# Gate of a quantised feed forward by tanh, one chunk pair at a time, and its weights rounded in pieces

## The chip, the cores and the metric

The kernel runs on one core of one Trainium2 chip. The metric is the device time of one execution in microseconds (us), lower is better. Each version is run several times and the median counts. The engines are TensorE (PE in the profile, with its weight loads as PEld), VectorE (DVE), ScalarE (ACT), GpSimd (POOL) and SyncE (SP), which here only issues transfers. Every engine works through its own instructions strictly in order and waits for others by semaphores.

## The reference, cut to what matters

Six blocks transform `x` of shape (4, 1024, 256), each followed by a residual add and a layer norm: self attention, cross attention and a feed forward in layer 0, then the same three kinds in layer 1. The change touches the feed forward of layer 0 alone:

```python
def act_quant(x):
    scale = 127.0 / jnp.clip(jnp.max(jnp.abs(x), axis=-1, keepdims=True), 1e-05)
    return jnp.clip(jnp.round(x * scale), -128, 127) / scale

def weight_quant(w):
    scale = 1.0 / jnp.clip(jnp.mean(jnp.abs(w)), 1e-05)
    return jnp.clip(jnp.round(w * scale), -1, 1) / scale
...
h = bit_linear(x, w1)                       # 256 -> 1024, both sides rounded
h = depthwise_conv1d(h.transpose(0, 2, 1), conv_w, conv_b)   # 3 taps along the sequence
h = h.transpose(0, 2, 1)
h = jax.nn.silu(h)
return bit_linear(h, w2)                    # 1024 -> 256, both sides rounded
```

So for each batch element `b`: the 1024 tokens are rounded with one scale per token, multiplied by a ternary weight, convolved along the sequence for each of the 1024 hidden channels, gated by silu, rounded again with one scale per token (the largest absolute value over the 1024 channels) and multiplied by a second ternary weight. silu(h) = h * sigmoid(h) = (h/2) * (1 + tanh(h/2)).

## The kernel before, in words

**Stages.** From 0 to about 780 us runs the self attention of layer 0, from there to about 1480 us its cross attention, to about 1890 us the self attention of layer 1, and then layer 1's cross attention and feed forward. The feed forward of layer 0 has no stage of its own. It is laid between the work of two others: batch elements 0 and 1 inside the cross attention (`wide_cross_attention`), 2 and 3 mostly inside the self attention of layer 1 (`wide_self_attention`).

**Order of the work.** Each stage collects events, `at(when, function, ...)`, sorts them by `when` and calls them. In the cross attention one unit of `when` is one call of `scores` (L706, L710 and L714: the maximum, four exponentials, the reciprocal; then the normalising on POOL, L718 and L721). Everything that goes to TensorE is pinned to this order (`pe`, `mm`); so are transfers that go through `pe`. Other instructions are placed by a planner: it issues what it expects to be ready, in its own estimate of time, and may move an early-ready instruction ahead of others on its engine. Once placed, the order on each engine is fixed.

**Weights.** `weight_quant` loads a weight as 128 x 2048 float32 (L616, into the slot `gt`, of which there is one), sums absolute values (L618, DVE), adds over the partitions with a matmul (L620, PE), takes the scale (L622, L624) and rounds to -1, 0 or 1 in three steps: L625 and L626 on DVE, L627 on POOL. It runs as one event at 20.5 for the first weight and at 36.5 for the second. The second load needs the slot that the first rounding leaves.

**Feed forward.** `schedule` spreads a batch element over a length of 38 to 40 units in four quarters `r` of 256 tokens. In `hidden(r, m)`, `m` from 0 to 3, TensorE makes two chunks of 128 channels; DVE takes them out of PSUM with the token scales (`ht`, L882, two buffers); for each chunk ACT does the middle tap with bias (L889) and DVE the two outer taps on 255 columns (L892, L895). `gated(r)` does the whole quarter at once: it adds the neighbours' taps at the two edges (L903, L905, from `ed` made in `edge_tokens`), takes silu of 128 x 2048 (L906, ACT) and the largest absolute value over the eight chunks (L908, DVE). `hidden_scales` turns these maxima (L915, PE) and makes scales (L917, L802 to L807); `quantised_hidden` multiplies and rounds (L923, L927, L930); `fed_forward` multiplies by the second weight. The quarter lies in the one slot `gt`, from `hidden` to L930.

In the stretches that the feed forward lies in, other ACT work is mostly exponentials: L710 in cross attention and L1036 in self attention. DVE's other work there is chiefly the maxima L706 and L1034 and the copies out of PSUM, L736, L1048.

Of the kernel before, what the change touches and what calls it, by code (L numbers as in the profile page):

```python
# [8 lines left out]
F32 = mybir.dt.float32  # L9
# [20 lines left out]
def decoder_kernel(ctx: ExitStack, tc: tile.TileContext, a: dict, out: bass.AP):  # L30
# [558 lines left out]
    def wide_cross_attention(wk, wf, slot, bank):  # L589
# [21 lines left out]
        def weight_quant(name):  # L611


            w = wf.tile([P, 8, E], F32, tag="gt", name="wf", bufs=1).rearrange("p c n -> p (c n)")
            src = a[name].rearrange("(c p) n -> p c n", p=P)
            nc.sync.dma_start(out=w.rearrange("p (c n) -> p c n", c=src.shape[1]), in_=src)  # L616
            asum = small.tile([P, 1], F32, tag="asum", name="asum")
            nc.vector.tensor_reduce(asum, w, AX.X, ALU.add, apply_absolute_value=True)  # L618
# [4 lines left out]
            sc = small.tile([P, 1], F32, tag="wsc", name="wsc")  # L623
# [3 lines left out]
            nc.gpsimd.tensor_scalar(wq.rearrange("p c n -> p (c n)"), w, -1.0, 0.0, ALU.max, ALU.add)  # L627
# [136 lines left out]
        at(20.5, weight_quant, "L0_ffn_w1")  # L764
        at(36.5, weight_quant, "L0_ffn_w2")
# [23 lines left out]
    def feed_forward(wf, bank):  # L789
# [4 lines left out]
        scs, dqs, xqTs, rows, edges, gts, ams, sc2s, dq2s, gqs, sts = ({} for _ in range(11))  # L794
# [52 lines left out]
        def edge_tokens(b):  # L847
# [3 lines left out]
            for hc in range(8):  # L851
# [3 lines left out]
            ed = edges[b] = wf.tile([P, 8, 3, 2], F32, tag="ed", name="ed", bufs=1)  # L855
# [3 lines left out]
                ed.rearrange("p c q n -> p c (q n)"),  # L859
# [3 lines left out]
            for n in range(2):  # L863
                nc.vector.tensor_tensor(
                    ed[:, :, :, n], ed[:, :, :, n],
                    cw[:, :, 2 * n : 2 * n + 1].to_broadcast([P, 8, 3]), ALU.mult,
                )

        def hidden(b, r, m):
            if m == 0:  # L870
                gts[b, r] = wf.tile([P, 8, N], F32, tag="gt", name="gt", bufs=1)
            g2 = gts[b, r]
            t = bank()
            for i in range(2):
# [709 lines left out]
```

## Time and profile before

| what | value |
|---|---|
| median of 3 runs | 2347.14 us (2345.06 to 2352.85) |
| the profiled execution | 2353.62 us, of which the profile's span is 2351.9 us |
| PE busy | 2202.1 us, 94% of the span |
| DVE busy | 1471.0 us, 63% |
| ACT busy | 1110.5 us, 47% |
| POOL busy | 504.6 us, 21% |
| mean granted TensorE clock | 0.957 of full speed |

The page's second part cuts the span into 40 slices and gives each engine's busy share in tenths; `PEclk` is the clock that was granted to TensorE. The table by stretches gives, for each stretch, its length, then busy us and the number of instructions for PE, PEld, DVE, ACT and POOL, then the granted clock, the share of the DMA engines and GB/s. A row of instruction groups reads: line, engine, operation, output<-input by the program's names, shapes, count | busy us in total, mean ns of one | idle time of the engine just before them and what ended it. In the time line, a row is start, duration, engine, line, operation, names, shapes, count, and in brackets the idle time before it. Matmul ends are modelled, so a busy PE can still be a PE that runs below its peak.

### The profile page before, as it was taken

How to read it: one execution, taken by the hardware profiler on the slowest of the kernel's cores; microseconds unless marked ns; L12 is line 12 of the kernel's file. 1: busy time of each engine (PE TensorE's matmuls, PEld its weight loads, DVE VectorE, ACT ScalarE, POOL GpSimd, SP SyncE). 2: the span in 40 equal slices, each digit the busy share in tenths (PEclk: the TensorE clock that was granted, in tenths of full speed). 3: DMA queues.
4: the chain of work that ended last, by engine and by line, in shares of the span. 5: the costliest groups of instructions: out<-in, count | busy, mean ns of one | idle time of the engine just before them, and what ended most of it. 6: DMA issues, size and time to landing. Idle time of an engine off the chain costs nothing.

```text
span 2351.9 us, 37670 instructions
## 1 busy us (share of the span) xinstructions
PE 2202.1 (94%) x14228; PEld 1288.3 (55%) x14228; DVE 1471.0 (63%) x3113; ACT 1110.5 (47%) x2699; POOL 504.6 (21%) x1111
## 2 busy tenths in 40 slices
PE   7999999999999999999889988889899999999996
PEld 4444544454444556556556555656666655555645
DVE  5666666666665654557787787775874365645544
ACT  1455554554555464445655654334543334444444
POOL 1111111111111464544334333000000021111102
PEclk9999999999999999999989988999999999999998
DMA  3201200000000100000000000000000010010101
GB/s 91 51 6 33 55 5 15 10 15 15 9 12 1 37 19 1 1 1 1 1 1 1 32 1 21 1 1 1 1 0 1 1 20 12 12 28 12 30 1 36
DMA packets 24437, 34.76 MB, mean 15 GB/s; under 512 B 5952, under 2 KB 19648, under 8 KB 24256
## 3 DMA queue, kind: packets, MB, share of 16 engines
q1 hardware_dynamic: 22640, 31.20, 5.8%
q8 instruction: 113, 1.85, 0.3%
q10 hardware_dynamic: 1616, 1.16, 0.2%
q14 instruction: 68, 0.56, 0.1%
HBM read 15.56 MB, written 4.19 MB: 8 GB/s over the span
## 4 chain that ended last, share of the span: by engine, by line
PE 74%; DVE 16%; ACT 7%; issue 1%; DMA 1%; POOL 1%; SPq 0%; ACTq 0%; DVEq 0%; POOLq 0%
PE s L178 22%; PE t L568 16%; PE s L1138 10%; PE s L568 9%; PE acc L178 6%; PE acc L1138 3%; PE t L735 2%; ACT u L710 2%; DVE gt L892 2%; DVE gt L895 2%; DVE x L156 1%; DVE bnst L136 1%; DVE am L908 1%; DVE nmp L319 1%; ACT gt L906 1%
## 5 line engine op out<-in xcount | busy, mean ns | idle before, releaser
L385 ACT ACTIVATE p<-s 128x512 f32<-128x512 f32 (+1 forms) x640 | 319.4, 554 | 297.4 <-PE s L178 294.7
L319 DVE TENSOR_REDUCE nmp<-s 128x1 f32<-128x512 f32 (+3 forms) x640 | 298.9, 524 | 155.7 <-PE s L178 155.7
L178 PE MATMUL s<-qs,kp 32*128 32x512 f32 (+3 forms) x1536 | 370.5, 532 | 2.7 <-DVE nmp L319 2.7
L178 PE MATMUL s<-kp,qp 32*128 32x128 f32 (+3 forms) x2304 | 329.5, 408 | 5.6 <-DVE nmp L319 3.5
L718 POOL TENSOR_SCALAR p<-u,rs 128x128 f32<-128x128 f32 x512 | 201.3, 411 | 339.1 <-DVE rs L714 242.9
L178 PEld LDWEIGHTS s<-kp,qp 32*128 32x128 f32 x2304 | 167.7, 188 | 142.9 <-issue 43.5
L388 POOL TENSOR_SCALAR_AFFINE_SELECT p<-p 128x256 f32<-128x256 f32 x256 | 100.6, 408 | 650.8 <-ACT p L385 650.8
L710 ACT ACTIVATE u<-s,nmx 128x154 f32<-128x154 f32 x512 | 192.1, 389 | 62.0 <-DVE nmx L706 50.5
L178 PEld LDWEIGHTS s<-qs,kp 32*128 32x128 f32 x1536 | 143.8, 187 | 65.4 <-DVE nmp L319 28.0
L141 POOL TENSOR_TENSOR rstd<-ve,neghalf 128x4 f32<-128x4 f32 (+1 forms) x56 | 54.7, 977 | 549.7 <-DVE ve L139 514.4
L178 PE MATMUL acc<-p,v 128*32 128x512 f32 (+3 forms) x1536 | 165.4, 511 | 1.1 <-ACT ot L427 0.8
L568 PEld LDWEIGHTS s<-kt,qt 64*128 64x128 f32 x1024 | 106.9, 194 | 77.7 <-issue 58.4
L568 PE MATMUL s<-kt,qt 64*128 64x154 f32 x1024 | 141.5, 325 | 2.1 <-ACT u L710 1.8
L706 DVE TENSOR_REDUCE nmx<-s 128x4 f32<-128x616 f32 x128 | 101.5, 793 | 62.5 <-PE s L568 62.0
L568 PE MATMUL t<-xT,xw 128*128 128x512 f32 x256 | 128.9, 628 | 4.0 <-DVE xT L638 3.7
L1295 DVE TENSOR_REDUCE nmt<-s 128x3 f32<-128x462 f32 (+1 forms) x192 | 99.0, 579 | 46.5 <-PE s L1138 46.5
L568 PE MATMUL t<-xw,ot 128*128 128x256 f32 x512 | 119.2, 387 | 4.3 <-DVE pt L736 3.8
L568 PE MATMUL t<-v,pt 128*128 128x256 f32 x512 | 117.9, 383 | 5.2 <-DVE pt L1048 3.8
L568 PE MATMUL s<-qt,xT 128*128 128x512 f32 x256 | 117.7, 603 | 0.0
L335 DVE TENSOR_REDUCE nmp<-s 128x4 f32<-128x512 f32 x128 | 82.6, 688 | 49.6 <-PE s L178 49.6
L568 PEld LDWEIGHTS t<-v,pt 128*128 128x128 f32 x512 | 96.8, 192 | 26.9 <-issue 5.7
L568 PEld LDWEIGHTS t<-xw,ot 128*128 128x128 f32 x512 | 96.8, 194 | 18.1 <-DVE pt L736 4.3
(255 smaller groups left out, 3898.6 us busy)
## 6 DMA issues: line engine op xcount, KB each, us to landing
qp<-sq SPq DMA_DIRECT2D x128, 64.0 KB, 2.3
kp<-sk SPq DMA_DIRECT2D x64, 64.0 KB, 2.3
out_dram<-x SPq DMA_DIRECT2D x8, 512.0 KB, 2.9
x<-in_x_dram SPq DMA_DIRECT2D x3, 1024.0 KB, 5.4
wf<-in_L_ffn_w_dram SPq DMA_DIRECT2D x2, 1024.0 KB, 5.2
xw<-in_L_xattn_wk_dram SPq DMA_DIRECT2D x1, 1024.0 KB, 5.3
xw<-in_L_xattn_wq_dram SPq DMA_DIRECT2D x1, 1024.0 KB, 5.8
xw<-in_L_xattn_wv_dram SPq DMA_DIRECT2D x1, 1024.0 KB, 5.1
```

Of the source, the lines that this page charges most:

```text
L141: nc.gpsimd.tensor_tensor(rstd[:, :n], ve[:, :n], neghalf[:, :n], ALU.pow)
L178: pe(nc.tensor.matmul(o, l, r, start=start, stop=stop))
L319: nc.vector.tensor_reduce(nmp[:, 2 * pair + g, qc, i : i + 1], t[g][:, c0 : c0 + n], AX.X, ALU.max)
L335: nc.vector.tensor_reduce(nmp[:, 2 * pair + g, q0 : q0 + 4, 0], t[g].rearrange("p (j n) -> p j n", j=4), AX.X, ALU.max,)
L385: nc.scalar.activation(p[:, g, :total], t[g][:, :total], AF.Exp)
L388: nc.gpsimd.affine_select(out=v, in_=v, compare_op=ALU.is_ge, fill=0.0, base=0, pattern=[[0, 2], [1, P]], channel_multiplier=-1,)
L568: pe(nc.tensor.matmul(o, l, r, start=start, stop=stop))
L706: nc.vector.tensor_reduce(nmx.rearrange("p i g -> p g i"), t, AX.X, ALU.max, negate=True)
L710: nc.scalar.activation(u[:, 2 * i + g, :], t[:, g, i, :], AF.Exp, bias=nmx[:, i, g : g + 1], accum_out=ssum[:, i, g : g + 1],)
L718: nc.gpsimd.tensor_scalar(p[:, h * P : (h + 1) * P], u[:, h, :P], rs[:, h : h + 1], 1.0, ALU.mult, ALU.mult)
L1138: pe(nc.tensor.matmul(o, l, r, start=start, stop=stop))
L1295: nc.vector.tensor_reduce(nmts[s % 2][:, 3 * u : 3 * u + n, g, 17], ts[g][:, : n * LK].rearrange("p (c k) -> p c k", k=LK), AX.X, ALU.max, ...
```

## The change

Four things change, all in the feed forward of layer 0.

1. **Weights.** `weight_quant` becomes four functions. The load is pinned in order on SP (events 12.6 and 28.6 instead of 20.5 and 36.5). The sum is four pieces of 512 columns, the mean adds four columns of PSUM, and the rounding is four pieces of three instructions, all on DVE; POOL has no part in it. Sums, mean and pieces have events of their own, one unit apart.
2. **Edges.** `ed` becomes ten columns per chunk (the neighbours of each quarter's two edges, with zeros at the ends of the sequence), cleared by POOL once per batch element. ACT copies two of them to the sides of each `ht`, which grows by two columns, so the convolution's outer taps run over all 256 columns and the edge additions (L903, L905) and the products L864 go.
3. **Gate.** The taps and bias are halved once. ACT takes tanh of each chunk pair at the end of `hidden`; `gated(r, m)`, one and a half steps later, does (tanh + 1) * g on DVE, an absolute value on ACT and a running maximum on DVE, with one more maximum of the two halves after the last pair. `ht` is kept as the place for tanh and the absolute value, so it is held until that pair's maximum. The maxima move from the slot `am` into the slot `xq`.
4. **Times.** For batch elements 2 and 3 the four `hidden` calls are 2.0 instead of 1.6 hundredths of the length apart.

```diff
-        def weight_quant(name):
...
-            nc.sync.dma_start(out=w.rearrange("p (c n) -> p c n", c=src.shape[1]), in_=src)
-            asum = small.tile([P, 1], F32, tag="asum", name="asum")
-            nc.vector.tensor_reduce(asum, w, AX.X, ALU.add, apply_absolute_value=True)
-            t = bank()
-            pe(nc.tensor.matmul(t[:, 0:1], ones, asum, start=True, stop=True))
-            wq, mean = quantised[name]
-            nc.vector.tensor_scalar(mean, t[:, 0:1], 1.0 / (P * 2048), 1e-5, ALU.mult, ALU.max)
+        floats = {}
+        def weight_loaded(name):
             w = wf.tile([P, 8, E], F32, tag="gt", name="wf", bufs=1).rearrange("p c n -> p (c n)")
...
+            pe(nc.sync.dma_start(out=w.rearrange("p (c n) -> p c n", c=src.shape[1]), in_=src))
+            asum = small.tile([P, 4], F32, tag="asum", name="asum")
             sc = small.tile([P, 1], F32, tag="wsc", name="wsc")
+            floats[name] = w, asum, sc
+        def weight_sum(name, i):
+            w, asum, _ = floats[name]
+            nc.vector.tensor_reduce(
+                asum[:, i : i + 1], w[:, i * 512 : (i + 1) * 512], AX.X, ALU.add, apply_absolute_value=True
+            )
+        def weight_mean(name):
+            _, asum, sc = floats[name]
+            t = bank()
+            pe(nc.tensor.matmul(t[:, 0:4], ones, asum, start=True, stop=True))
+            _, mean = quantised[name]
+            nc.vector.tensor_reduce(mean, t[:, 0:4], AX.X, ALU.add)
+            nc.vector.tensor_scalar(mean, mean, 1.0 / (P * 2048), 1e-5, ALU.mult, ALU.max)
             nc.vector.reciprocal(sc, mean)
+        def weight_quant(name, i):
+            w, _, sc = floats[name]
+            w = w[:, i * 512 : (i + 1) * 512]
+            wq = quantised[name][0].rearrange("p c n -> p (c n)")[:, i * 512 : (i + 1) * 512]
             nc.vector.tensor_scalar(w, w, sc, RND, ALU.mult, ALU.add)
             nc.vector.tensor_scalar(w, w, RND, 1.0, ALU.subtract, ALU.min)
-            nc.gpsimd.tensor_scalar(wq.rearrange("p c n -> p (c n)"), w, -1.0, 0.0, ALU.max, ALU.add)
+            nc.vector.tensor_scalar(wq, w, -1.0, 0.0, ALU.max, ALU.add)
...
-        at(20.5, weight_quant, "L0_ffn_w1")
-        at(36.5, weight_quant, "L0_ffn_w2")
+        for t0, name in ((12, "L0_ffn_w1"), (28, "L0_ffn_w2")):
+            at(t0 + 0.6, weight_loaded, name)
+            at(t0 + 9.6, weight_mean, name)
+            for i in range(4):
+                at(t0 + 5.6 + i, weight_sum, name, i)
+                at(t0 + 10.6 + i, weight_quant, name, i)
...
+        nc.vector.tensor_scalar(cw, cw, 0.5, None, ALU.mult)
+        nc.vector.tensor_scalar(cb, cb, 0.5, None, ALU.mult)
...
-            ed = edges[b] = wf.tile([P, 8, 3, 2], F32, tag="ed", name="ed", bufs=1)
+            ed = edges[b] = wf.tile([P, 8, 2 * Q + 2], F32, tag="ed", name="ed", bufs=1)
+            nc.gpsimd.memset(ed, 0.0)
...
-            for n in range(2):
-                nc.vector.tensor_tensor(
-                    ed[:, :, :, n], ed[:, :, :, n],
-                    cw[:, :, 2 * n : 2 * n + 1].to_broadcast([P, 8, 3]), ALU.mult,
-                )
...
-            ht = wf.tile([P, 2, N], F32, tag="ht", name="ht", bufs=2)
+            ht = wf.tile([P, 2, N + 2], F32, tag="ht", name="ht", bufs=2)
             nc.vector.tensor_tensor(
-                ht, t.rearrange("p (i n) -> p i n", i=2),
+                ht[:, :, 1 : N + 1], t.rearrange("p (i n) -> p i n", i=2),
...
+            for c, k in ((0, 2 * r), (N + 1, 2 * r + 3)):
+                nc.scalar.copy(ht[:, :, c : c + 1], edges[b][:, 2 * m : 2 * m + 2, k : k + 1])
+            g2 = gts[b, r][:, 2 * m : 2 * m + 2, :]
             for i in range(2):
                 hc = 2 * m + i
-                g = g2[:, hc, :]
+                g = g2[:, i, :]
                 nc.scalar.activation(
-                    g, ht[:, i, :], AF.Identity, bias=cb[:, hc : hc + 1], scale=cw[:, hc, 1:2]
+                    g, ht[:, i, 1 : N + 1], AF.Identity, bias=cb[:, hc : hc + 1], scale=cw[:, hc, 1:2]
                 )
-                nc.vector.scalar_tensor_tensor(
-                    g[:, 1:], ht[:, i, : N - 1], cw[:, hc, 0:1], g[:, 1:], ALU.mult, ALU.add
-                )
-                nc.vector.scalar_tensor_tensor(
-                    g[:, : N - 1], ht[:, i, 1:], cw[:, hc, 2:3], g[:, : N - 1], ALU.mult, ALU.add
-                )
-        def gated(b, r):
-            g = gts[b, r]
-            if r > 0:
-                nc.vector.tensor_tensor(g[:, :, 0], g[:, :, 0], edges[b][:, :, r - 1, 0], ALU.add)
-            if r < Q - 1:
-                nc.vector.tensor_tensor(g[:, :, N - 1], g[:, :, N - 1], edges[b][:, :, r, 1], ALU.add)
-            nc.scalar.activation(g, g, AF.Silu)
-            am = ams[b, r] = wf.tile([P, N], F32, tag="am", name="am", bufs=1)
-            nc.vector.tensor_reduce(
-                am, g.rearrange("p c n -> p n c"), AX.X, ALU.max, apply_absolute_value=True
-            )
+                for k in (0, 2):
+                    nc.vector.scalar_tensor_tensor(
+                        g, ht[:, i, k : k + N], cw[:, hc, k : k + 1], g, ALU.mult, ALU.add
+                    )
+            nc.scalar.activation(ht[:, :, :N], g2, AF.Tanh)
+            ths[b, r, m] = ht
+        def gated(b, r, m):
+            g2 = gts[b, r][:, 2 * m : 2 * m + 2, :]
+            th = ths.pop((b, r, m))
+            nc.vector.scalar_tensor_tensor(g2, th[:, :, :N], 1.0, g2, ALU.add, ALU.mult)
+            if m == 0:
+                ams[b, r] = wf.tile([P, 2, N], F32, tag="xq", name="am", bufs=1)
+            am = ams[b, r]
+            if m == 0:
+                nc.scalar.activation(am, g2, AF.Abs)
+            else:
+                nc.scalar.activation(th[:, :, :N], g2, AF.Abs)
+                nc.vector.tensor_tensor(am, am, th[:, :, :N], ALU.max)
+            if m == 3:
+                nc.vector.tensor_tensor(am[:, 0, :], am[:, 0, :], am[:, 1, :], ALU.max)
...
-                    on(u + (2.65 if inside else 1.6) * m, hidden, r, m)
-                on(u + (8.5 if inside else 6), gated, r)
+                    d = 2.65 if inside else 2.0
+                    on(u + d * m, hidden, r, m)
+                    on(u + d * (m + 1.5), gated, r, m)
```

More of the change, by code (lines that the diff above doesn't have):

```diff
@@ L609, in wide_cross_attention @@
         xTs, kts, vts, qts, pts, prs, ots, rss = {}, {}, {}, {}, {}, {}, {}, {}
-        def weight_quant(name):
+        floats = {}
+        def weight_loaded(name):
             w = wf.tile([P, 8, E], F32, tag="gt", name="wf", bufs=1).rearrange("p c n -> p (c n)")
             src = a[name].rearrange("(c p) n -> p c n", p=P)
-            nc.sync.dma_start(out=w.rearrange("p (c n) -> p c n", c=src.shape[1]), in_=src)
-            asum = small.tile([P, 1], F32, tag="asum", name="asum")
-            nc.vector.tensor_reduce(asum, w, AX.X, ALU.add, apply_absolute_value=True)
+            pe(nc.sync.dma_start(out=w.rearrange("p (c n) -> p c n", c=src.shape[1]), in_=src))
+            asum = small.tile([P, 4], F32, tag="asum", name="asum")
+            sc = small.tile([P, 1], F32, tag="wsc", name="wsc")
+            floats[name] = w, asum, sc
[6 more added lines that the diff above has]
+            _, asum, sc = floats[name]
             t = bank()
-            pe(nc.tensor.matmul(t[:, 0:1], ones, asum, start=True, stop=True))
-            wq, mean = quantised[name]
-            nc.vector.tensor_scalar(mean, t[:, 0:1], 1.0 / (P * 2048), 1e-5, ALU.mult, ALU.max)
-            sc = small.tile([P, 1], F32, tag="wsc", name="wsc")
+            pe(nc.tensor.matmul(t[:, 0:4], ones, asum, start=True, stop=True))
+            _, mean = quantised[name]
+            nc.vector.tensor_reduce(mean, t[:, 0:4], AX.X, ALU.add)
+            nc.vector.tensor_scalar(mean, mean, 1.0 / (P * 2048), 1e-5, ALU.mult, ALU.max)
             nc.vector.reciprocal(sc, mean)
+        def weight_quant(name, i):
+            w, _, sc = floats[name]
+            w = w[:, i * 512 : (i + 1) * 512]
+            wq = quantised[name][0].rearrange("p c n -> p (c n)")[:, i * 512 : (i + 1) * 512]
             nc.vector.tensor_scalar(w, w, sc, RND, ALU.mult, ALU.add)
             nc.vector.tensor_scalar(w, w, RND, 1.0, ALU.subtract, ALU.min)
-            nc.gpsimd.tensor_scalar(wq.rearrange("p c n -> p (c n)"), w, -1.0, 0.0, ALU.max, ALU.add)
+            nc.vector.tensor_scalar(wq, w, -1.0, 0.0, ALU.max, ALU.add)
         def x_transposed(b, e, q):
@@ L793, in feed_forward @@
         cb = load(a["L0_ffn_conv_b"], [P, 8], "cb", pool=wf)
-        scs, dqs, xqTs, rows, edges, gts, ams, sc2s, dq2s, gqs, sts = ({} for _ in range(11))
+        nc.vector.tensor_scalar(cw, cw, 0.5, None, ALU.mult)
+        nc.vector.tensor_scalar(cb, cb, 0.5, None, ALU.mult)
+        scs, dqs, xqTs, rows, edges, gts, ams, sc2s, dq2s, gqs, ths = ({} for _ in range(11))
         Q = 4
@@ L858, in edge_tokens @@
             nc.vector.tensor_tensor(
-                ed.rearrange("p c q n -> p c (q n)"),
+                ed[:, :, 2 : 2 * Q],
                 t[:, :64].rearrange("p (c n) -> p c n", c=8)[:, :, :6],
@@ L871, in hidden @@
                 gts[b, r] = wf.tile([P, 8, N], F32, tag="gt", name="gt", bufs=1)
-            g2 = gts[b, r]
             t = bank()
@@ L914, in hidden_scales @@
             for j in range(2):
-                pe(nc.tensor.transpose(t[:, j * P : (j + 1) * P], ams[b, r][:, j * P : (j + 1) * P], ident))
+                pe(nc.tensor.transpose(t[:, j * P : (j + 1) * P], ams[b, r][:, 0, j * P : (j + 1) * P], ident))
             amax = small.tile([P, 2], F32, tag="amax2", name="amax2", bufs=2)
```

## The prediction

> **What bounds the kernel now.** I read the page's slices first, then the table by stretches where the feed forward lies, then the groups of instructions there, the waits, and the time line around the dips. A word on measuring: 0.3% of this kernel, about 7 us, is what can be told from no change.
>
> The first view, the slices (each about 59 us), shows TensorE busy nearly throughout, with its weak part and its lower granted clock in slices 18 to 31, where the feed forward is laid between other work.
>
> ```profile
> PE   7999999999999999999889988889899999999996
> PEclk9999999999999999999989988999999999999998
> ```
>
> The second view is the table by stretches of 20 us: PE, PEld, DVE, ACT and POOL busy, then the clock. Two stretches contain the weights' rounding, the others lie at gates of batch elements 0 and 1. Read PE's busy time and the clock together.
>
> ```profile
> 880.00:900.00 20.00, 16.21 (x78) 11.32 (x76) 9.24 (x16) 6.30 (x28) 7.07 (x21) 0.83 0.07 24
> 940.00:960.00 20.00, 15.56 (x86) 9.13 (x84) 15.70 (x23) 8.14 (x37) 14.40 (x17) 0.99 0.00 1
> 960.00:980.00 20.00, 19.87 (x103) 11.03 (x103) 8.77 (x20) 9.92 (x41) 6.98 (x21) 0.92 0.00 0
> 1120.00:1140.00 20.00, 13.51 (x72) 7.18 (x71) 13.99 (x26) 13.45 (x37) 6.29 (x17) 0.85 0.01 2
> 1220.00:1240.00 20.00, 16.37 (x67) 9.20 (x67) 18.88 (x32) 11.86 (x39) 6.78 (x18) 0.74 0.00 1
> 1440.00:1460.00 20.00, 13.59 (x55) 6.80 (x55) 13.77 (x20) 10.96 (x32) 6.25 (x19) 0.70 0.01 2
> ```
>
> The third view, the groups by line, gives the prices: the gate (L906, its table load, L908) and what restores the exponential table behind it (L710's and L1036's loads).
>
> ```profile
> L908 DVE TENSOR_REDUCE am<-gt 128x256 f32<-128x2048 f32 x16 | 58.3, 3644 | 21.7 <-ACT gt L906 21.6
> L906 ACT ACTIVATE gt<-gt 128x2048 f32<-128x2048 f32 x16 | 30.6, 1910 | 1.1 <-DVE gt L903 0.9
> L906 ACT ACT_TABLE_LOAD x15 | 19.2, 1283 | 13.5 <-DVE gt L905 6.8 <-DVE gt L903 6.6
> L710 ACT ACT_TABLE_LOAD x8 | 10.3, 1283 | 0.1
> L1036 ACT ACT_TABLE_LOAD x7 | 9.0, 1283 | 1.0 <-DVE nmx L1034 0.9
> ```
>
> The fourth, DVE's waits up to 1000 us, holds one long wait: the second weight's sum, queued early on DVE, waits for a load that cannot start before POOL has rounded the first. The time line's other two rows show POOL's rounding, and a DVE step that takes 1.44 us at 1123 us and 6.89 us beside it.
>
> ```profile
> DVE asum L618 <- DMA wf<-in_L_ffn_w_dram: 7.2, 1, 7.2
> 951.13 7.08 POOL L627 TENSOR_SCALAR L_ffn_w<-wf 128x2048 bf16<-128x2048 f32 x1
> 952.59 6.89 DVE L156 TENSOR_SCALAR x<-x,bnmv,rstd 128x256 f32<-128x256 f32 x4
> ```
>
> **A. Weights.** In the three stretches from 880 to 980 above PE is idle 3.79 + 4.44 + 0.13 = 8.4 us, and the clock's shortfall is (0.17 + 0.01 + 0.08) x 20 = 5.2 us. Together 13.6 us is the most that can come back here. Gone: 2 x 7.08 us on POOL, which stands in front of the softmax's normalising (L718, about 0.37 us each) and of TensorE's transposes behind it, and with it DVE's stretched L156. Added on DVE per weight: four sums at about 0.69 (L319 takes 0.685 for 512 columns) for one of 2.28; twelve pieces of 512 columns at an estimated 0.48 (between L156's 0.36 for 256 and L626's 1.22 for 2048) for 1.29 + 1.22; one small reduction, 0.17. That is 8.7 for 4.8, so +3.9, or 7.8 us for both, beside DVE work of 9 to 11 us in 20 once the stalled stretch is left out; the cover is TensorE's 10 us of waiting room there. I charge 3. The second load still waits for the last piece, is past no other SP transfer in this stretch, and lands in 5.2; if the planner again puts its first sum early, DVE waits up to that, with L706 and L736 behind it and ACT's exponentials behind L706. If all covers fail, A costs 7.8 + 5.2 - 7.2 = +6. Sum: -13.6 + 3, or about -10; range -14 to +6. Halving `cw` and `cb` is two instructions of 0.17; were they queued before their loads land, DVE would wait about 2 us (786.1 to 788.5, by the 2.3 of the spread's loads) near 787, where PE idles 3.65 anyway. The POOL memset of 80 columns is under the 0.63 of a 640-column one (L595), four times.
>
> **B and C, the work itself.** Per quarter DVE loses L908 (3.64) and the edge steps (about 0.3), and gains four gate steps at 0.69 (L479: 128x512, both inputs in SBUF), three maxima at 0.69 (same row) and one of 256 columns, about 0.47: 5.3 for 3.9, so +1.4, over 16 quarters +22 us. The outer taps on 256 for 255 columns cost nothing visible. ACT loses 30 loads x 1.283 = 38.5 and silu's 30.6, and gains 64 tanh at 0.60 (L1438's row), 64 absolute values at about 0.61, and 128 copies of 2 columns at no more than 0.2 (L1262's copy of 64 columns: 0.203): 39 + 39 + 26 for 69, so +35. tanh needs no load: L1438 has no table load among its rows, though exponentials lie around it. So the change saves no engine any work; it takes away one block of 1.28 + 1.91 + 1.28 = 4.47 us on ACT and one of 3.64 on DVE, ahead of which exponentials and L706 wait, and spreads small pieces instead. On DVE the idle 21.6 us waiting for silu goes, against the 22 us added.
>
> The Trainium skill ("ScalarE: Activation LUTs", What ACT_TABLE_LOAD costs) puts a switch at about 2.66 us, a drain included. The rows here show 1.283 and a next instruction 0.02 us after it (1074.36 to 1075.66): the trace does not show the drain. By the page's figure the freed time would be 80 us and ACT would come out lighter, not heavier, by about 6 us (an estimate).
>
> **B. Batch elements 0 and 1 (1040 to 1480 us).** Nearly every low stretch follows a gate: PE idle sums to 33 us in those, and the clock's shortfall to 42 us. They overlap, so a second measure: the stretch from L706's start at 1039.84 to that at 1449 has 71 units. Undisturbed units take 3.22 us (825 to 850 us); out-projections add 3.5 each, 18 of them; the batch element's transposes, keys and values about 13 twice; the feed forward's matmuls about 24 us (an estimate from its rows) twice, less an unfinished part: 229 + 62 + 29 + 45 = 365. The lost time is 409 - 365 = 44 us, 5.5 per quarter. What comes back is unknown: nothing, if DVE's in-order waits take its place; all 44, if the gate's block makes them all. DVE is busy 162 of the 200 us to 1400, so it is nearly as full as TensorE; I take half, 22, and charge half of DVE's extra 8 x 1.4: -22 + 5 = -17, range -44 to +30 (below).
>
> **C. Batch elements 2 and 3.** The chain runs here through DVE alone for some 16 us ahead of a gate, then load, silu, L908 (6.86 us, 1556.1 to 1563.0), then L915. After the change the chain behind the last tap is tanh, gate, absolute value, two maxima: 0.60 + 0.69 + 0.61 + 0.69 + 0.47 = 3.1. But the earlier pairs' three gate steps and two maxima (5 x 0.69 = 3.5) now lie on DVE ahead of the last gate step: 6.9 - 3.1 - 3.5 = 0.3 gained where DVE sets the pace, 3.8 where not. PE waited for L908 10.1 us in all over 1500 to 1800 us. Half of that: -5, range -15 to +10.
>
> **Sum.** -10 - 17 - 5 = -32. The profiled execution took 2353.6 (span 2351.9), so 2321.6; it lies 6.5 above the median, and against the median 2347.1 I forecast 2315.
>
> **Rivals.**
>
> *Slower: two buffers of `ht` and the waits between ACT and DVE.* Now `ht` is free after the last tap. Afterwards it is held through tanh, gate, absolute value and maximum; the chain from L882 to there is 0.68 + 0.4 + 1.2 + 2.0 + 0.60 + 0.69 + 0.61 + 0.69 = 6.9 us without queueing, and the next pair but one (L882, behind it the bank that TensorE needs, with transposes and L706 behind) waits for it. In batch elements 2 and 3 pairs are 2 hundredths of about 40 units of 3.6, 2.9 us apart, so two buffers give 5.8 for 6.9. If every maximum waits just its absolute value out, DVE loses 64 x 0.61 = 39 and 22 of work less 21.6 of old waiting; with A's 10 gained that is +29, 2376; half passed on gives +15, 2362. It decides where the mean wait per pair goes beyond 32 / 64 = 0.5 us on the path. For it: ACT already waits 43 us for L882. Against: exponentials and copies lie between to fill it. The Trainium skill ("GPSIMD Engine Reference", its specification table: SBUF interfaces shared with VectorE, contention with two-port modes and two SBUF inputs) speaks on this side: both new DVE kinds read two SBUF inputs. The trace agrees in the weight's case (6.89 for 1.44); by it the 42 us of such steps in B could each stretch L718 when they meet. Chance 0.26.
>
> *The clock comes back: a larger gain.* The clock is 0.66 to 0.85 in stretches behind gates and 1.00 between. If the pieces leave no hole long enough, B's 44 return whole and C's 10: -10 - 44 - 10 = -64, 2283. The Trainium skill ("TensorE: Matmul & The Clock Gate", Part 1) has a gate that halves the clock after an idle window of about 3.4 us; the trace's holes of 3.2 to 5.8 us and stretches at 0.74 agree. Chance 0.14.
>
> *The gate was hidden by DVE's load anyway.* B and C give nothing, A its 10: 2337. For it: DVE's work does not shrink. Against: the dips sit at the gates. Chance 0.20. *Nothing at all:* A's sum waits again and the rest cancels, within 7 us: 0.08.
>
> **How the numbers follow.** Forecast case 0.32, and it is the likeliest: 2315. Faster by over 0.3%: 0.32 + 0.14 + 0.20 = 0.66; within: 0.08; slower: 0.26. Half of the larger gains lie below 2280 (0.07), and a third of the slower cases above 2364 (0.09); the range is 2280 to 2364. The forecast case alone spans 2300 to 2328.
>
> **What would show it.** No table load but the first; POOL without L627's 7.08 and PE full from 880 to 980; no DVE wait for the second load; clock of 0.9 or more behind gates. Wrong it would be if DVE's maxima show long waits for the absolute values, if L882 waits for them and PE for L882, or if DVE is over 17 of 20 us and PE still dips.

## The result, and the profile after

The changed kernel takes 2306.73 us in the median of 4 runs (2302.96 to 2311.27), the kernel before 2348.98 us in runs taken beside it (2345.06 to 2352.85). The ratio is 0.9825, 95% interval 0.9808 to 0.9841: 42 us or 1.75% faster. The profiled executions took 2305.49 us (span 2303.8) and 2353.62 us, so 48.1 us apart; the mean granted clock is 0.971 after 0.957.

First the page's slices. What was the weak part of before, slices 18 to 31, has become three eights and a seven, and the clock is below nine tenths in one slice besides the last.

```profile
PE   7999999999999999999999998879989999999996
PEclk9999999999999999999999999989999999999998
```

Then the table by stretches (length, busy us of PE, PEld, DVE, ACT, POOL, granted clock, DMA share, GB/s). The first three rows are the stretches of the prediction's term A, the fourth and fifth lie at gates. The first four have the times of rows that the prediction shows of before; but the changed kernel is 14 us ahead at the start of B and 50 at its end, so the fourth holds somewhat later work.

```profile
880.00:900.00 20.00, 20.00 (x117) 13.60 (x116) 11.88 (x23) 10.27 (x45) 10.45 (x27) 1.00 0.00 1
940.00:960.00 20.00, 19.05 (x110) 11.03 (x108) 14.57 (x36) 11.66 (x50) 10.63 (x29) 1.00 0.00 1
960.00:980.00 20.00, 20.00 (x109) 12.14 (x106) 10.04 (x21) 10.18 (x43) 7.30 (x22) 1.00 0.00 2
1120.00:1140.00 20.00, 19.31 (x117) 12.01 (x115) 16.75 (x36) 12.37 (x47) 7.86 (x18) 1.00 0.00 1
1180.00:1200.00 20.00, 15.86 (x79) 7.86 (x77) 19.64 (x45) 13.54 (x51) 11.39 (x25) 0.91 0.00 1
```

The prediction has three terms, and each has its own stretch of the time line. I cut at the starts of VectorE's maxima, which both kernels issue in the same number and order: number 16, 56 and 127 of the cross attention (counted from 0; line 706 before, 723 after) and the last of layer 1's self attention (1034 and 1062). Before, these start at 850.78, 1039.84, 1449.01 and 1882.76 us. After, by the time line (start, duration, engine, line, operation, idle time before it):

```profile
850.02 0.80 DVE L723 TENSOR_REDUCE nmx<-s 128x4 f32<-128x616 f32 x1 [0.51 <-PE s L568]
...
1025.51 0.80 DVE L723 TENSOR_REDUCE nmx<-s 128x4 f32<-128x616 f32 x1 [5.05 <-PE s L568]
...
1399.45 0.80 DVE L723 TENSOR_REDUCE nmx<-s 128x4 f32<-128x616 f32 x1
...
1834.79 1.23 DVE L1062 TENSOR_REDUCE nmx<-s 128x1 f32<-128x1024 f32 x1 [2.60 <-PE s L568]
```

Stretch A (the weights) goes from 189.06 to 175.49 us, **-13.6**. Stretch B (batch elements 0 and 1) goes from 409.17 to 373.94, **-35.2**. Stretch C (2 and 3) goes from 433.75 to 435.34, **+1.6**. All of the gain lies in A and B.

In B the clock has come back with the shorter holes. By the table by stretches, of before and then of after:

```profile
1040.00:1449.00 409.00, 375.17 (x2036) 237.50 (x2035) 310.63 (x626) 233.96 (x794) 160.15 (x375) 0.91 0.03 8
```

```profile
1026.00:1399.00 373.00, 352.51 (x2030) 225.13 (x2030) 314.29 (x665) 238.44 (x895) 174.97 (x379) 0.98 0.03 9
```

PE idle falls from 33.8 to 20.5 us, and the clock's shortfall from 0.09 x 409 = 37 to 0.02 x 373 = 7 us. TensorE's list of waits in B fits that: before, its longest waits were 5.8, 3.6, 3.5 and 3.2 us; after, none is longer than 2.8. (Columns: who waited <- for whom: us in all, times, the longest.) Before:

```profile
PE t L568 <- DVE qt L690: 6.7, 2, 3.5
PE t L568 <- ACT vr L676: 5.8, 1, 5.8
PE t L915 <- DVE am L908: 3.6, 1, 3.6
PE t L738 <- ACT pr L739: 3.2, 1, 3.2
```

After:

```profile
PE t L950 <- DVE sc L829: 3.0, 2, 2.8
PE t L755 <- ACT pr L756: 2.4, 3, 1.0
PE t L568 <- DVE pt L753: 2.1, 2, 1.1
```

The clock is lost in spells at half speed. Cut at their ends, the table by stretches has 0.50 from 1079.2 to 1089.5 us and in six more spells of 10.2 to 10.3 us up to 1417.2 before, and after in one of 10.2 us from 1358.8 and one of 3.4 us from 1191.5. By TensorE's time line all but the last of these begin during a hole of 2.0 to 5.8 us in its work. The Trainium skill ("TensorE: Matmul & The Clock Gate", Part 1) says that an idle window of about 3.4 us halves the clock. The half agrees, the length of the holes only on the whole: the spell from 1222.6 begins in a hole of 2.0 us, and the one from 1191.5, which makes the 0.91 above, follows holes of at most 1.05.

The groups of instructions by line give the prices of the new operations. The only table load left is the kernel's first (line 237).

```profile
L927 DVE SCALAR_TENSOR_TENSOR gt<-ht,gt 128x512 f32<-128x512 f32 x64 | 44.2, 690 | 4.2 <-ACT ht L920 3.5
...
L920 ACT ACTIVATE ht<-gt 128x512 f32<-128x512 f32 x64 | 40.3, 630 | 41.5 <-DVE gt L917 36.3 <-DVE rs L731 2.2 <-DVE bnmv L137 1.2
...
L935 DVE TENSOR_TENSOR am<-am,ht 128x512 f32<-128x512 f32 x48 | 33.7, 702 | 3.4 <-ACT ht L934 3.2
...
L934 ACT ACTIVATE ht<-gt 128x512 f32<-128x512 f32 x48 | 30.2, 630 | 6.1 <-DVE gt L927 6.1
...
L908 ACT COPY ht<-ed 128x2 f32<-128x2 f32 x128 | 19.5, 198 | 12.7 <-DVE am L935 7.0 <-POOL ed L881 5.0 <-DVE ed L884 0.5
...
L937 DVE TENSOR_TENSOR am<-am 128x256 f32<-128x256 f32 x16 | 7.1, 445 | 0.2
```

### The profile page after: what moved, and what is told of

The parts are those of the page before. It is cut to its first block, busy times and chain, and to the rows that moved or that the text cites. A ratio compares the mean times of both kernels' runs of the same rounds, so it can differ in the third digit from the quotient of the medians.

```text
span 2303.8 us, 38032 instructions
## 1 busy us (share of the span) xinstructions
PE 2172.9 (94%) x14228; PEld 1275.8 (55%) x14228; DVE 1482.0 (64%) x3223; ACT 1127.3 (49%) x2909; POOL 507.7 (22%) x1113
## 4 chain that ended last, share of the span: by engine, by line
PE 73%; DVE 19%; ACT 5%; issue 1%; POOL 1%; DMA 1%; SPq 0%; ACTq 0%; DVEq 0%; POOLq 0%
PE s L178 22%; PE t L568 15%; PE s L1166 10%; PE s L568 9%; PE acc L178 6%; DVE gt L917 4%; PE acc L1166 3%; PE t L752 2%; ACT u L727 2%; DVE bnst L136 1%; DVE x L156 1%; DVE nmp L319 1%; DVE nmx L723 1%; PE t L1075 1%; DVE ht L903 1%
## 5 line engine op out<-in xcount | busy, mean ns | idle before, releaser
L735 POOL TENSOR_SCALAR p<-u,rs 128x128 f32<-128x128 f32 x512 | 214.5, 437 | 290.5 <-DVE rs L731 196.1
L568 PE MATMUL s<-kt,qt 64*128 64x154 f32 x1024 | 136.5, 316 | 0.5 <-ACT qt L709 0.3
L568 PE MATMUL t<-xT,xw 128*128 128x512 f32 x256 | 122.4, 601 | 7.5 <-DVE xT L655 4.4
L917 DVE SCALAR_TENSOR_TENSOR gt<-ht,cw,gt 128x256 f32<-128x256 f32 x256 | 117.9, 501 | 6.6 <-ACT gt L913 5.5
```

The costliest lines, as they stand in the source:

```text
L568: pe(nc.tensor.matmul(o, l, r, start=start, stop=stop))
L735: nc.gpsimd.tensor_scalar(p[:, h * P : (h + 1) * P], u[:, h, :P], rs[:, h : h + 1], 1.0, ALU.mult, ALU.mult)
L917: nc.vector.scalar_tensor_tensor(g, ht[:, i, k : k + N], cw[:, hc, k : k + 1], g, ALU.mult, ALU.add)
```

## The experiments

All lengths of A, B and C are cut at the same maxima as above, and differences are to the kernel before. How far a stretch moves without cause can be read from kernels with the same instructions in it. A differs by 1.5 us among the nine with the change's weights (-12.5 to -14.0). B differs by 5.7 among the six with the change's gate there (changed kernel, after_again, gate_only, mixed_max, pool_product, pt_on_scalar: -30.7 to -36.4), and C by 3.0 among the first three of these. The kernel before moves too: weights_only and round_on_vector have its gate, and their B is 2.5 and 2.4 us shorter than in its one profile. So the change itself is worth 28 to 36 us in B, and comparisons with it are given as ranges.

| kernel | A | B | C | median, us | ratio (95%) |
|---|---|---|---|---|---|
| changed kernel | -13.6 | -35.2 | +1.6 | 2306.73 | 0.9825 (0.9808 to 0.9841) |
| weights_only | -12.5 | -2.5 | +0.6 | 2333.17 | 0.9933 (0.9910 to 0.9956) |
| round_on_vector | -12.5 | -2.4 | +0.5 | 2330.27 | 0.9924 (0.9898 to 0.9951) |
| gate_only | +2.0 | -36.4 | -0.5 | 2316.30 | 0.9862 (0.9829 to 0.9895) |
| no_load | -0.2 | -27.7 | -15.1 | 2308.95 | 0.9835 (0.9800 to 0.9869) |
| half_tanh | -0.2 | -2.6 | +6.0 | 2351.60 | 1.0014 (1.0001 to 1.0026) |
| loads_back | -13.9 | -25.5 | +14.9 | 2325.56 | 0.9907 (0.9883 to 0.9931) |
| max_at_once | -13.9 | -22.9 | -3.8 | 2309.25 | 0.9836 (0.9819 to 0.9853) |
| no_gate_step | -12.7 | -38.4 | -13.5 | 2284.96 | 0.9739 (0.9718 to 0.9759) |
| mixed_max | -12.5 | -30.7 | -1.5 | 2304.91 | 0.9804 (0.9777 to 0.9830) |
| pool_product | -14.0 | -32.5 | +12.2 | 2311.36 | 0.9842 (0.9816 to 0.9867) |
| pt_on_scalar | -14.0 | -32.4 | -5.9 | 2297.91 | 0.9791 (0.9772 to 0.9810) |
| after_again | -14.0 | -36.3 | -1.4 | 2300.04 | 0.9798 (0.9769 to 0.9828) |

### The same kernel once more

> The changed kernel itself beside the two above on one chip: 40 to 46 us faster than the kernel before, 13.6 of it ahead of batch element 0, 35 in 0 and 1, none in 2 and 3.

No edit. Its median is 2300.04 us, 49.6 below the kernel before in runs beside it, more than the 40 to 46 expected. B and C differ from the first profile by 1.1 and 3.0 us. The two profiled executions differ by 14.8 us, of which 10.5 lie ahead of A (850.0 and 839.6 us), where hardly anything of the change runs; so the stretches tell two kernels apart better than whole times do. The 6.7 us between the two medians is also what two kernels must differ by before one is called better.

### The weights alone

`weights_only` is the kernel before with the first part of the change: the four functions, the pinned loads and the events one unit apart.

```diff
-        at(20.5, weight_quant, "L0_ffn_w1")
-        at(36.5, weight_quant, "L0_ffn_w2")
+        for t0, name in ((12, "L0_ffn_w1"), (28, "L0_ffn_w2")):
+            at(t0 + 0.6, weight_loaded, name)
+            at(t0 + 9.6, weight_mean, name)
+            for i in range(4):
+                at(t0 + 5.6 + i, weight_sum, name, i)
+                at(t0 + 10.6 + i, weight_quant, name, i)
```

> The kernel before with the new weight code alone (pinned load, sums and rounding in four pieces, all on VectorE). By the start of token_scales for batch element 0 the changed kernel is 13.6 us ahead of the kernel before. If the weights alone make that, this kernel is 13 to 14 us faster, about 2335, and stays ahead by the same amount to the end. If the gate's part has a share in it (another order on the engines), it is less than 10 us faster. The second weight's sum does not wait for its load in either case.

`round_on_vector` is the kernel before with one word changed; the sum stays whole, early and unpinned.

```diff
-            nc.gpsimd.tensor_scalar(wq.rearrange("p c n -> p (c n)"), w, -1.0, 0.0, ALU.max, ALU.add)
+            nc.vector.tensor_scalar(wq.rearrange("p c n -> p (c n)"), w, -1.0, 0.0, ALU.max, ALU.add)
```

> The kernel before with one word changed: the last rounding step (L627) on VectorE instead of GpSimd, whole, 128x2048. If GpSimd's 7.08 us block is the cause, both the stretched L156 and VectorE's wait of 7.2 us for the second load shrink, and this alone gives 10 to 14 us (2333 to 2337). If it is the pieces and the later sums that count, the second weight's sum still waits for its load (up to 5.2 us), and the gain is 5 to 9 us.

A shortens by 12.5 us in both, and the medians are 2333.17 and 2330.27. So the engine of the last rounding step is the cause, and pieces, pinned loads and later sums add nothing that can be measured. The time line of round_on_vector shows the step at 1.30 us where POOL took 7.08, and the early sum waiting 0.50 us for the second load where it waited 7.2; the slot comes free sooner. It also shows a POOL group of four normalisings that takes 2.46 us beside VectorE's rounding (1.43 for the group at 854.89), with no loss that can be seen.

```profile
858.18 2.46 POOL L718 TENSOR_SCALAR p<-u,rs 128x128 f32<-128x128 f32 x4 [1.54 <-DVE rs L714]
858.56 1.22 DVE L626 TENSOR_SCALAR wf<-wf 128x2048 f32<-128x2048 f32 x1
...
860.41 1.30 DVE L627 TENSOR_SCALAR L_ffn_w<-wf 128x2048 bf16<-128x2048 f32 x1
...
867.02 2.29 DVE L618 TENSOR_REDUCE asum<-wf 128x1 f32<-128x2048 f32 x1 [0.50 <-DMA wf<-in_L_ffn_w_dram]
```

### The gate alone

`gate_only` is the changed kernel with the old `weight_quant` and its two events: the diff of weights_only the other way round.

> The changed kernel with the weights done as before (whole, last step on GpSimd). If the parts add up, it is 42 - 13.6 = 28 to 33 us faster than the kernel before (2314 to 2319): 35 in batch elements 0 and 1, 2 lost in 2 and 3. If they help each other, it is under 25 faster.

A is +2.0, B -36.4, C -0.5. The two parts of the change sit in their own stretches: in A this kernel lacks the 12.5 to 14, and in B and C it has what the whole change has.

### The table loads alone

`no_load` takes the loads away from the kernel before and leaves the block of the gate, the whole maximum and the edges as they were. It does not compute silu: the multiplication is left out.

```diff
-            nc.scalar.activation(g, g, AF.Silu)
+            nc.scalar.activation(g, g, AF.Tanh)
```

> The kernel before with tanh in place of silu in the one instruction L906 and nothing else, so the multiplication of the gate is left out and every duration stays, but no table has to be loaded. Theory 1, the table loads (2 x 1.28 us in front of and behind silu) make the holes at the gates: 20 to 35 us faster (2313 to 2328), the clock 0.9 or more in the stretches behind gates. Theory 2, the block as a whole (1.91 us on ScalarE and 3.64 us on VectorE in one piece) makes them: at most 10 us faster (2338 or more), and the clock still falls to 0.8 or less behind most gates.

B falls by 27.7 and C by 15.1 us: 42.8 us for 30 loads of 1.283 us, which is 1.43 us for each. The medians have 39.5 us, more than the 20 to 35 expected if the loads make the holes. In B the 16 loads, 20.5 us long, are worth more than their own time, in C the 14 of 18.0 us less. (Against the B of round_on_vector the sum is 40 us, or 1.34 per load.) In B the clock goes with them: the table by stretches has 0.96 for 0.91, with 22.3 us of PE idle for 33.8.

```profile
1036.00:1418.00 382.00, 359.70 (x2041) 230.89 (x2038) 309.37 (x627) 213.15 (x779) 161.41 (x377) 0.96 0.03 9
1418.00:1837.00 419.00, 392.06 (x1778) 271.13 (x1778) 276.18 (x583) 151.53 (x246) 21.93 (x34) 0.97 0.00 1
```

The Trainium skill ("ScalarE: Activation LUTs", What ACT_TABLE_LOAD costs) has 2.66 us for a switch, a drain of 1.38 us included. Here the rows show the load's 1.283, and what its removal is worth is nearer to that than to the page's figure, which would have made it 30 x 2.66 = 80 us.

### The same gate as one block

`half_tanh` has silu by tanh, so no loads, but at the place of the old gate: two halves of the quarter, and the whole maximum behind them.

```diff
-            nc.scalar.activation(g, g, AF.Silu)
+            for k in (0, 4):
+                th = wf.tile([P, 4, N], F32, tag="gq", name="th", bufs=1)
+                nc.scalar.activation(th, g[:, k : k + 4, :], AF.Tanh)
+                nc.vector.scalar_tensor_tensor(
+                    g[:, k : k + 4, :], th, 1.0, g[:, k : k + 4, :], ALU.add, ALU.mult
+                )
```

(and the two halvings of `cw` and `cb`, as in the change).

> The kernel before with the gate by tanh and no table load, but the gate still as one block per quarter: tanh and (tanh + 1) * g in two halves of 128x1024 (the place for tanh is the slot gq), then the one maximum L908; weights as before. Against the run without loads (42.8 us won from the cross attention's start on, 27.7 of it in batch elements 0 and 1, 15.1 in 2 and 3) VectorE has 16 x 2.5 = 40 us more to do. Theory 1, the loads are the whole matter and the pieces none: a loss of at most 10 against that in batch elements 0 and 1, so 18 or more won there. Theory 2, VectorE's work is on the path one for one: about 8 won in 0 and 1 (27.7 - 20), and 2 and 3 lose 5 (15.1 - 20). The pair by pair form won 36 in 0 and 1; if it is the pieces that make the rest, this one stays under 20 there.

The kernel is no faster than before: 2351.60 us, ratio 1.0014 (1.0001 to 1.0026). Against no_load it loses 25.1 us in B and 21.1 in C, 46 in all, for 39.7 us of added VectorE work in a longer block (both halves use one buffer, so the second tanh waits for the first product: 4.8 us in all):

```profile
L911 DVE SCALAR_TENSOR_TENSOR gt<-th,gt 128x1024 f32<-128x1024 f32 x32 | 39.7, 1240 | 11.8 <-ACT th L910 11.6
```

So tanh for silu at the old place wins nothing by itself. The loads' 43 us are paid back on VectorE, unless the work is laid out as the change does: against half_tanh the changed kernel is 32.6 us shorter in B and 4.4 in C. Besides the pieces it has the running maximum, which is tested below, and the new edges, which have no run of their own.

### The loads put back into the changed kernel

`loads_back` is the changed kernel with silu in place of tanh in the last pair of each quarter, so that the loads come back; it leaves out that pair's right gate.

```diff
-            nc.scalar.activation(ht[:, :, :N], g2, AF.Tanh)
+            nc.scalar.activation(ht[:, :, :N], g2, AF.Silu if m == 3 else AF.Tanh)
```

> The changed kernel with silu in place of tanh in the last chunk pair of each quarter (the gate's product is then not silu; only the table loads are meant): about 30 loads of 1.28 us come back, each for a block of 0.63 instead of 1.91 us. If a load costs what its absence won in the kernel before (42.8 / 30 = 1.4 us each), this kernel is 40 to 45 us slower than the changed one, about where the kernel before is less the weights' 13. If in pieces the loads are hidden, it loses less than 15.

The groups by line have the 30 loads again, in three rows:

```profile
L920 ACT ACT_TABLE_LOAD x15 | 19.2, 1283 | 8.2 <-DVE gt L917 8.1
...
L727 ACT ACT_TABLE_LOAD x8 | 10.3, 1283 | 0.1
...
L1064 ACT ACT_TABLE_LOAD x7 | 9.0, 1283 | 0.1
```

Against the changed kernel's first profile B is 9.8 us longer (5 to 11 by the range) and C 13.3 (16.3 against after_again), 23 us in all or 0.77 per load. Neither expectation came, 40 to 45 or under 15. It is about half of what the loads cost before the change, and the saving lies in B: 16 loads for 9.8 us, where no_load found 27.7 for as many. In B the block that they frame is 0.63 us of ACT here and was 1.91, so ACT has its other work back after 3.2 us and not 4.5; that this is the reason is not shown.

### The whole maximum in place of the running one

```diff
             if m == 3:
-                nc.vector.tensor_tensor(am[:, 0, :], am[:, 0, :], am[:, 1, :], ALU.max)
+                am = ams[b, r] = wf.tile([P, 2, N], F32, tag="xq", name="am", bufs=1)
+                nc.vector.tensor_reduce(
+                    am[:, 0, :], gts[b, r].rearrange("p c n -> p n c"), AX.X, ALU.max, apply_absolute_value=True
+                )
```

(the absolute values and the three running maxima of a quarter go).

> The changed kernel with the maxima not kept as chunks come: gate by pairs as changed, but no absolute values on ScalarE and no running maxima, and one reduction of 128x2048 on VectorE (3.64 us) after the last pair. VectorE's work per quarter goes from 2.5 to 3.6 us, ScalarE loses 2.5 us, and ht is free right after the gate step. If the waits between the engines and the two buffers of ht are what eats the gain in batch elements 2 and 3, they now win some 8 us or more there. If VectorE's amount of work is what counts, 2 and 3 lose about 9 (8 x 1.1) and 0 and 1 some 5 to 10.

B is 12.3 us longer than in the changed kernel's first profile (8 to 14 by the range), C shorter by 5.4 or 2.4 by the changed kernel's two profiles; so neither the 8 or more expected there of shorter waits came, nor the loss of 9 expected of more work on VectorE. B is still 20.3 us shorter than in half_tanh, which is what the pieces and the new edges win there without the running maximum. `mixed_max` therefore keeps the running maximum for batch elements 0 and 1 and takes the whole one for 2 and 3:

```diff
+            if b >= 2:
+                if m == 3:
+                    am = ams[b, r] = wf.tile([P, 2, N], F32, tag="xq", name="am", bufs=1)
+                    nc.vector.tensor_reduce(
+                        am[:, 0, :], gts[b, r].rearrange("p c n -> p n c"), AX.X, ALU.max, apply_absolute_value=True
+                    )
+                return
```

> The changed kernel, but for batch elements 2 and 3 the maxima at once by one reduction, as in max_at_once; 0 and 1 as changed. By the stages' sums (0 and 1: -35 as changed; 2 and 3: -3.8 in max_at_once against +1.6 as changed) it is 5 us faster than the changed kernel, if the form in one part does not move the other. If what max_at_once won in 2 and 3 only came from where 0 and 1 had left off, within 2 us of the changed kernel.

C comes out at -1.5, the same as in after_again, and the median at 2304.91, between those of the changed kernel's two measurements. In B the running maxima are worth 8 us or more; in C the two forms can't be told apart.

### The gate step left out

```diff
-            nc.vector.scalar_tensor_tensor(g2, th[:, :, :N], 1.0, g2, ALU.add, ALU.mult)
...
-                nc.scalar.activation(am, g2, AF.Abs)
+                nc.scalar.activation(am, th[:, :, :N], AF.Abs)
...
-                nc.scalar.activation(th[:, :, :N], g2, AF.Abs)
+                nc.scalar.activation(th[:, :, :N], th[:, :, :N], AF.Abs)
```

> The changed kernel without the step (tanh + 1) * g (L927 left out; absolute values and maxima of tanh itself). VectorE loses 64 x 0.68 = 44 us of work, the rest of the order stays. If VectorE's amount of work sets the pace in batch elements 2 and 3, they win 15 us or more, as the run without loads did; if ScalarE's waits and the order do, under 8. In batch elements 0 and 1: under 10 either way, since little lost time is left there.

VectorE loses 32 x 0.69 = 22 us of work in each of B and C, and each pair's chain gets 0.69 us shorter. B gains 2 to 8 us over the changed kernel, C 15.1 or 12.1. In B the gate's steps on VectorE are largely hidden; in C they cost more than half their length. Whether there it is VectorE's work or the chain's length, this run can't tell, as it takes both away. By the table by stretches, C of the kernel before, of the changed kernel and of this one (VectorE 276 us in 434, 283 in 436 and 264 in 420; PE idle 37.7, 40.2 and 32.4). The clock of C has not come back with the change:

```profile
1449.00:1883.00 434.00, 396.35 (x1777) 273.21 (x1778) 275.98 (x582) 169.75 (x259) 22.58 (x36) 0.96 0.00 1
```

```profile
1399.00:1835.00 436.00, 395.79 (x1783) 275.13 (x1781) 283.34 (x624) 181.70 (x368) 25.01 (x34) 0.96 0.00 1
```

```profile
1389.00:1809.00 420.00, 387.64 (x1775) 269.84 (x1774) 264.37 (x589) 182.19 (x365) 24.39 (x34) 0.98 0.00 1
```

### The product on POOL

`pool_product` is mixed_max with the gate step of batch elements 2 and 3 split between ACT (tanh + 1) and POOL, which is busy for only 22 us of C in mixed_max.

```diff
+            else:
+                nc.scalar.activation(th[:, :, :N], th[:, :, :N], AF.Copy, bias=1.0)
+                nc.gpsimd.tensor_tensor(g2, th[:, :, :N], g2, ALU.mult)
```

> mixed_max, and for batch elements 2 and 3 the gate's product goes off VectorE: ScalarE adds 1 to tanh (about 0.63 us per pair) and GpSimd multiplies (about 1.27 per pair, by the row of the last stage's 128x512 addition). VectorE loses 8 x 2.7 = 22 us in that stretch. If VectorE's work sets the pace there (no_gate_step won 15 in 2 and 3 for 22), it is 8 to 15 us faster than mixed_max. If GpSimd's access to the memory stretches VectorE's own steps, or the longer chain from the last tap to the maximum counts, it is no faster or slower.

C is 13.7 us longer than in mixed_max, though VectorE has 22 us less to do. The view of the tile `gt` from 1400 to 1840 us says what came in its place (first row: minimum/median/maximum ns, then first and last start; the others: who waited for the gate's instructions, us and times):

```profile
L931 POOL TENSOR_TENSOR gt<-ht,gt x32: 1172/1184/1426, 1425.7 to 1718.1; 128x512 f32<-128x512 f32 x32
...
  PE t L953: 16.7, 4
...
  ACT ht L908: 12.7, 16
...
  DVE am L935: 9.8, 6
...
  DVE ht L903: 3.8, 3
```

The step takes 1.18 us on POOL instead of 0.69, with 0.63 on ACT ahead of it. The maximum waits for it, TensorE waits for the maximum, and `ht` comes free later, so that the next pairs' edge copies and L903 wait too. The chain behind the last tap counts, and not VectorE's load alone. POOL also stretches VectorE's steps, as the other half of the expectation had it, by less: the 128 taps of C are busy for 58.8 us, where mixed_max has 55.1. This is the wait for the two buffers of `ht` that the prediction feared, seen here with a chain 1.1 us longer per pair.

### A copy moved from VectorE to ACT

`pt_on_scalar` is the changed kernel with half of the copies at L1076, in the stretch of the feed forward, moved to ACT.

```diff
-                (nc.vector.tensor_copy, nc.scalar.copy)[q](
+                (nc.scalar.copy if q or 8 * b + c < 20 else nc.vector.tensor_copy)(
```

> The changed kernel, with the first half of each transposed p copied out by ScalarE too (L1076), for the 20 chunks of layer 1's self attention beside which the feed forward runs: VectorE loses 20 x 0.68 = 14 us there, ScalarE gains 20 x 0.58 = 12, and nothing of the gate's own chain changes. If VectorE's work paces batch elements 2 and 3 (22 us less of it won 13.5 there, in the run without the gate's product), 5 to 9 us faster than the changed kernel. If it is the gate's chain that paces them, within 3 us of it, or slower where exponentials wait behind the copies.

C is -5.9, so 4.5 to 7.5 us below the changed kernel's two profiles, but B, whose instructions are the same, is 3 to 4 us longer than in them. The median of 2297.91 can't be told from 2300.04. Whether VectorE's relief in C is worth anything that lasts stays open, and no kernel of the study that computes the whole feed forward beats the changed one clearly.

## Why the prediction was right, step by step

The forecast was faster, 2315 us, with 2280 to 2364 as the range. 2306.73 lies in the range and in the forecast case's own span (2300 to 2328), 8 us below the number. The sum of -32 was -47 over the three stretches and -42 between the medians. Its three terms were off in both directions.

**A, -10: right in its cause, mis-sized by the charge of 3.** Measured were -13.6, -14.0 and, by itself, -12.5: the whole 13.6 us that the prediction named as the most that can come back. PE fills the three stretches (20.00, 19.05, 20.00 of 20) and the clock is at 1.00. (The L156 group at 1123 us, which the prediction puts at 1.44 us, takes 1.52 in the time line.) VectorE's added work, charged with 3 us, cost nothing that can be seen. The table of before had already shown why: 9 to 11 us of VectorE in 20, once the stalled stretch is left out. round_on_vector narrows the cause to the engine of one step.

**B, -17: right in its cause, mis-sized by the half.** The prediction estimated 44 us of lost time, took half of it because VectorE seemed nearly as full as TensorE, and charged 5 for VectorE's extra work. (Its sum has 29 where 13 twice is 26; with 26 the estimate is 47.) Measured were 28 to 36 us (35.2 in the first profile), two thirds to four fifths of the 44 with nothing more charged. So the step that failed is the choice of a half from an average: VectorE was busy in 314 of 373 us, and the added pieces still found room, since no_gate_step shows 22 us of them to be worth only 2 to 8. In B the mechanism is that of the rival *the clock comes back*: the shortfall went from 37 to 7 us. Taking away the loads alone shortens B by 27.7 us (no_load). The prediction had entered them as 38.5 us of ACT time and as part of a block, and never priced them as a path of their own.

**C, -5: nothing came.** +1.6 and -1.4 us lie within the 3 us that two profiles of one kernel differ by. The prediction had 0.3 us per quarter gained where VectorE sets the pace and 3.8 where not, and took half of PE's wait for L908. What the runs show is the balance: the removed loads are worth 15.1 us in C (no_load), and the gate's steps alone cost 12 to 15 there (no_gate_step), so the one pays for the other. TensorE still waits for the maxima in C. By its list of waits, before from 1500 to 1800 us, the view that the prediction used:

```profile
PE t L915 <- DVE am L908: 10.1, 4, 3.4
PE t L568 <- DVE gq L930: 7.5, 3, 4.1
```

After, from 1460 to 1760 us, where L942 is what was L915:

```profile
PE t L942 <- DVE am L937: 10.9, 3, 5.5
PE t L568 <- DVE gq L957: 8.3, 3, 4.6
```

That is 10.9 us after for 10.1 before: the wait stayed and changed its name. Over the whole of C it is 4.8 us in no_load and 4.5 in no_gate_step. In the 16 us up to the end of each of the three waits VectorE is busy for 16.0, 13.3 and 15.1 us (before, at its four, for 14.7, 12.4, 13.9 and 13.9). This fits the first of the prediction's two cases, VectorE as the pace, but does not show it: mixed_max gives VectorE 9 us more to do in C and loses nothing, and pool_product gives it less and loses. The later `hidden` calls too lie in C alone, and no run is without them. So why C gained nothing stays in part open.

**The sizes.** Tanh was put at 0.60 us and took 0.63, the absolute value at 0.61 and took 0.63, the gate step at 0.69 and took 0.69, the running maximum at 0.69 and took 0.70, the last maximum at 0.47 and took 0.45, the edge copies at no more than 0.2 and took 0.198. Tanh needs no load beside exponentials, as said. "Saves no engine any work" holds, and nearly in size: with each instruction at its own duration, ACT's work rose by 35.4 us (forecast 35) and VectorE's by 22.9 (forecast 22 for the gate and 7.8 for the weights). The busy times rose by less, ACT from 1110.5 to 1127.3 us and VectorE from 1471.0 to 1482.0, since instructions in a row overlap and busy time counts the overlap once: the 128 edge copies are 25.3 us by their mean and 19.5 busy. One reduction on VectorE was named and not counted: L156's twelve steps between 780 and 990 us fell from 10.0 to 4.6. The outer taps on 256 columns cost nothing visible, as said: their mean is 501 ns, and 498 on 255.

**The slower rival** needed 0.5 us of wait per pair on the path. VectorE's waits for ACT in the gate, from 1000 to 1800 us, are 6.7 us in all, 0.1 per pair:

```profile
DVE gt L927 <- ACT ht L920: 3.5, 8, 0.8
DVE am L935 <- ACT ht L934: 3.2, 9, 1.0
```

The old wait for silu, 21.6 us, is gone, and `ht` is waited for in the edge copies alone, 7.0 us behind L935 in the groups above. What was feared of POOL in B did come, without a loss that can be told: the table by stretches has 175 us of POOL there for 160 with nearly as many instructions, and its normalising takes 468 ns for 427. Without the gate step (no_gate_step) it is 167 us and 439 ns, so VectorE's new steps are what stretches it. POOL is busy for less than half of B. The Trainium skill's rule on the shared SBUF interfaces ("GPSIMD Engine Reference", its specification table) agrees with that in its sign. The weight's case, which the prediction counts for this rule, is a step with one tensor input (L156), so it is B that bears on the two inputs. **Gate hidden** (2337) falls with gate_only, **nothing at all** with the result.

## What to carry to other kernels

Price a block on the path by what waits behind it on its engine, and test it by taking the suspected instruction away alone: here 30 table loads were worth 40 to 43 us, a little more than their own 38.5. Removing them by a longer formula gained nothing until the formula was cut into pieces that fit between other work (with new edges, whose share is not known), and then it gained in one stretch and not in the next. So estimate each stretch by itself, and not by an engine's busy share: VectorE was busy for 84% of B and 65% of C, yet a step that was nearly free in B (22 us of VectorE for 2 to 8) cost more than half its length in C.

## What the runs showed of the hardware

- A table load of 1.283 us cost 1.43 us of kernel time in the old layout (1.73 in B, 1.08 in C) and 0.77 in the new one (0.61 in B, 0.95 in C), each by one profile against one. In B the granted clock moves with the loads: 0.91 with them, 0.96 without.
- The clock is lost in spells at 0.50, of 3.4 and 10.2 to 10.3 us in B. It recovered from 0.91 to 0.98 there as the longest wait fell from 5.8 to 2.8 us, with VectorE, ACT and POOL all busier than before in a shorter time.
- VectorE and POOL stretch each other in both directions: L156's group of four took 6.89 us beside POOL's rounding, the first instruction alone 5.76, and 1.52 us at 1123 us; a POOL group of 1.43 us became 2.46 beside VectorE's rounding. With the rounding on POOL, which holds up the normalising and the second load as well, A was 12.5 us longer.
- A product of two float32 tensors of 128x512 took 1.18 us on POOL; the gate step of the same shape on VectorE, which also adds 1, took 0.69.
- Instructions in a row on one engine overlap: 128 copies of 198 ns on ACT keep it busy for 19.5 us and not 25.3, and 256 taps of 501 ns keep VectorE busy for 117.9 and not 128.2.
